# Product's norm: 8-KB pieces, first loads split by channel, the first three units' x gathered during the triangle

## The chip, the cores and the metric

The kernel runs on one core of a Trainium2 chip, in fp32 throughout. The metric is the device time of one execution in microseconds. The runs shown of the kernel before took 1777.58, 1777.96 and 1781.21 us; their median is 1777.96 us.

A core has TensorE (PE), VectorE (DVE), ScalarE (ACT), GpSimd (POOL) and SyncE (SP). Each runs its own instruction list in order. Transfers are started from the lists of SP, ACT and POOL and carried out by 16 DMA engines which all of them share.

## The reference

The input x is one 512 x 512 picture with 64 channels. Two layers follow each other. This change lies in the first one:

```
xn = layernorm(groupnorm(x))                       # over 64 channels
left, right = (xn @ w + b) * mask * sigmoid(...)   # mask[i, j] = m[i] * m[j], m is 0 or 1 per row
out = einsum('bkjd,bkid->bijd', left, right)       # the triangle product, one 512 x 512 product per channel d
out = layernorm(out, onorm_w, onorm_b)             # over d: the product's norm
out = out @ out_w + out_b
x   = x + out * sigmoid(xn @ ogate_w + ogate_b)
```

The second layer is a Fourier convolution that keeps 12 x 12 modes, after another group norm, added to x again. Rows and columns whose m is 0 have a product of zero, and after norm and projection a constant row there.

## The kernel before

At most K = 256 rows have m = 1, and the kernel ranks them first. The path that runs here is `compact`. Its stages, in order of time:

1. A first reading of x for the group norm's sums, and of the 256 x 256 compact part into on-chip memory (to about 300 us of the trace).
2. The sides: left and right are made and stored to DRAM in `left_d` and `right_d`, each [64 channels, 256, 256] (to 445 us).
3. **The triangle** (447 to 619 us): a loop over the 64 channels c. `load_sides(c + 6)` (L865) fetches a channel's two sides, 256 KB each, `turn_sides` (L873, PE) transposes them, `keep_sides` (L879 DVE, L883 ACT) takes them out of PSUM, `product(c)` (L895 PE, L900 DVE) multiplies and masks them, and L903 stores 256 KB to `tri_d` [64, 256, 256]. The sides have five buffers each; the output has four. SP issues the loads and the stores in the order of the code: store of c, then loads of c + 6. POOL has nothing to do in this stage.
4. **The product's norm** (621 to 752 us): `tri_d` holds channels outermost, the norm wants channels innermost. The work goes in 64 steps of 1024 (i, j) pairs. `load_product(q)` (L1025) fetches what two steps need, as two DMAs of 64 channels x 4 KB, into a ring of four buffers that fills place 6. `centered(s)` (L1058, PE) multiplies by a centering matrix and by the output weights at once, which also turns the data. ACT squares the one half (L1078) and copies the other (L1079). DVE sums the squares of two steps (L1083), ACT takes the root for 8 steps (L1089), DVE inverts it (L1263) and scales (L1271), POOL adds the output bias for two steps (L1278), and L1283 stores 512 KB, 4 KB for each partition, to `u_d`.
5. **The units** (750 to 1450 us): 32 units of 64 columns x 128 rows in 8 steps each. `load(k, r)` (L638, an indirect DMA from POOL, two of 1024 KB for each unit, one 8-KB row for each partition) gathers the unit's x; PE transposes and projects it (L1038, L1045), and the gate, the product from `u_d` (`load_u`, L1100, 32 DMAs from SP for each pair of units) and x are joined (L1109, L1113, POOL). L1129 stores the new x to `x1_h`; statistics and the forward transform go beside it.
6. The Fourier modes, and the last pass over x: gather, add, store (from 1450 us).

Stages 4 and 5 are one loop over s, written out by hand under `manual_schedule`: every engine's order is the order of the code, from s = -13 (LEAD) to the end. At step s, `centered` works for step s + 12 and the scaling (L1271) for step s. The gather of unit v + 3 is issued at steps 3 and 6 of unit v, so the gathers of units 0, 1 and 2 are issued in the last 24 steps of the norm. `first` is 8, the number of groups of 8 steps in the norm. A product load waits until PE has done with the buffer it refills; a store to `u_d` waits for POOL's addition; both are in SP's list.

`places` is one on-chip tensor of eight places of 16 KB per partition. x of unit k lies in place `order[k % 5]`, with order = (0, 1, 3, 4, 2). The data of `u_d` for a pair of units lies in place 5 or 6. Place 7 holds smaller things.

## Time and profile before

The profiled execution took 1777.78 us, 0.18 us under the median; its span is 1776.0 us, so 1.8 us lie around the span.

| Engine | busy us in the whole span | share |
|---|---|---|
| PE | 1567.8 | 88% |
| DVE | 1413.7 | 80% |
| ACT | 933.0 | 53% |
| POOL | 936.5 | 53% |

| Stage, us of the span | what runs there | DMA share | GB/s |
|---|---|---|---|
| 450 to 600 | triangle | 0.90 | 301 |
| 600 to 620 | end of the triangle | 0.60 | 209 |
| 640 to 676 | norm | 0.88 | 283 |
| 676 to 711 | norm | 1.02 | 345 |
| 711 to 733 | norm, first gathers of x | 0.92 | 328 |
| 900 to 1000 | units | 0.71 | 248 |
| 1580 to 1776 | last pass | 0.99 | 417 |

DMA share is the mean busy share of the 16 DMA engines in the stretch. The shares over the whole span say little about one stage, since the stages have different limits; the table by stretches of time is the view to begin with, and then the list of one engine's instructions in order of time, with the idle time ahead of each in square brackets and what ended it.

### The profile page before, as it was taken

How to read it: one execution, taken by the hardware profiler on the slowest of the kernel's cores; microseconds unless marked ns; L12 is line 12 of the kernel's file. 1: busy time of each engine (PE TensorE's matmuls, PEld its weight loads, DVE VectorE, ACT ScalarE, POOL GpSimd, SP SyncE). 2: the span in 40 equal slices, each digit the busy share in tenths (PEclk: the TensorE clock that was granted, in tenths of full speed). 3: DMA queues.
4: the chain of work that ended last, by engine and by line, in shares of the span. 5: the costliest groups of instructions: out<-in, count | busy, mean ns of one | idle time of the engine just before them, and what ended most of it. 6: DMA issues, size and time to landing. Idle time of an engine off the chain costs nothing. (4 is left out here: it accounts for less than half of the span.)

```text
span 1776.0 us, 32619 instructions
## 1 busy us (share of the span) xinstructions
PE 1567.8 (88%) x10918; PEld 1242.0 (70%) x10918; DVE 1413.7 (80%) x2982; ACT 933.0 (53%) x1660; POOL 936.5 (53%) x695
## 2 busy tenths in 40 slices
PE   6779799997999978899999999999999977998772
PEld 5667666662899867787888888888888745665341
DVE  7989678887455568688999999999999984865451
ACT  3666566663333266676777777777777742011000
POOL 4666211111000037698999999999999881111110
PEclk9999999999899999899999999999999976555555
DMA  7999278878898789868767767776776699999999
GB/s 281 386 386 388 107 206 227 229 229 245 279 305 303 257 246 347 298 196 296 265 242 257 253 233 259 264 249 239 249 264 244 212 318 400 425 427 427 426 427 385
DMA packets 192593, 518.48 MB, mean 292 GB/s; under 512 B 37664, under 2 KB 104480, under 8 KB 151456
## 3 DMA queue, kind: packets, MB, share of 16 engines
q1 hardware_dynamic: 156112, 295.65, 47.5%
q0 software_dynamic: 32832, 218.45, 33.4%
q10 hardware_dynamic: 3472, 2.20, 0.5%
q8 instruction: 89, 1.46, 0.3%
q14 instruction: 88, 0.72, 0.1%
HBM read 311.60 MB, written 204.60 MB: 291 GB/s over the span
## 5 line engine op out<-in xcount | busy, mean ns | idle before, releaser
L1045 PE MATMUL w_ps<-gate_x,xt_c 128*128 128x128 f32 x2048 | 280.5, 281 | 30.0 <-DVE z_t L1274 28.6
L1113 POOL TENSOR_TENSOR places<-places,z_t 128x1024 f32<-128x1024 f32 x127 | 301.3, 2372 | 8.0
L1045 PEld LDWEIGHTS w_ps<-gate_x,xt_c 128*128 128x128 f32 x2048 | 252.0, 194 | 46.4 <-DVE z_t L1274 44.6
L1045 PE MATMUL c_ps<-center_x,xt_c 128*128 128x128 f32 x2048 | 277.0, 279 | 0.8 <-ACT xt_c L1040 0.4
L1045 PEld LDWEIGHTS c_ps<-center_x,xt_c 128*128 128x128 f32 x2048 | 252.8, 194 | 3.8 <-ACT xt_c L1040 3.0
L1440 PE MATMUL l_ps<-places,rinv 24*128 24x512 f32 x512 | 206.2, 1118 | 29.3 <-DVE places L1447 19.0
L1168 DVE BATCH_NORM_STATS2 stats2c<-places 128x6 f32<-128x128 f32 x1024 | 220.5, 278 | 9.9 <-POOL places L1113 9.9
L1083 DVE TENSOR_REDUCE scratch<-sq_c 128x16 f32<-128x1024 f32 x160 | 194.6, 1216 | 31.1 <-ACT sq_c L1078 16.1
L1221 ACT ACTIVATE z_t<-z_t 128x1024 f32<-128x1024 f32 x128 | 135.5, 1058 | 131.8 <-DVE z_t L1280 131.1
L1440 PEld LDWEIGHTS l_ps<-places,rinv 24*128 24x128 f32 x512 | 119.8, 302 | 110.8 <-DVE places L1447 56.9
L1278 POOL TENSOR_TENSOR z_t<-z_t,bias_row_out 128x1024 f32<-128x1024 f32 x32 | 75.6, 2363 | 226.3 <-PE y_ps L1058 202.1
L1040 ACT ACTIVATE xt_c<-t_ps,ab_xc 128x512 f32<-128x512 f32 x256 | 176.0, 688 | 11.5 <-PE t_ps L1038 10.6
L1274 DVE TENSOR_TENSOR z_t<-w_ps,rs_n 128x512 f32<-128x512 f32 x256 | 172.0, 672 | 6.2 <-PE w_ps L1045 6.1
L1076 ACT ACTIVATE sq_c<-c_ps 128x512 f32<-128x512 f32 x256 | 150.8, 589 | 31.4 <-PE c_ps L1045 30.8
L1280 DVE TENSOR_TENSOR z_t<-z_t,scratch 128x1024 f32<-128x1024 f32 x128 | 156.3, 1221 | 9.9 <-ACT rs_n L1089 3.7
L688 DVE BATCH_NORM_STATS2 stats1c<-x_ps 128x6 f32<-128x512 f32 x256 | 157.1, 682 | 7.7 <-PE x_ps L687 7.4
L1109 POOL TENSOR_TENSOR z_t<-z_t,places 128x1024 f32<-128x1024 f32 x64 | 151.8, 2371 | 14.6 <-ACT z_t L1221 14.4
L1038 PE MATMUL t_ps<-c_ident,places 128*128 128x128 f32 x1024 | 158.4, 278 | 0.0
L1038 PEld LDWEIGHTS t_ps<-c_ident,places 128*128 128x128 f32 x1024 | 118.5, 142 | 51.4 <-issue 51.4
L1447 DVE TENSOR_TENSOR places<-places,l_ps 128x512 f32<-128x512 f32 x176 | 109.3, 682 | 55.2 <-DMA places<-x_h,dst_i 42.1
L1109 POOL TENSOR_TENSOR z_t<-z_t,bias_row_out 128x1024 f32<-128x1024 f32 x63 | 149.4, 2372 | 5.8 <-ACT z_t L1221 5.5
L673 ACT COPY xc<-xg 128x128 f32 x352 | 105.0, 298 | 66.1 <-POOL xc L673 47.1
(214 smaller groups left out, 2557.0 us busy)
## 6 DMA issues: line engine op xcount, KB each, us to landing
x_h<-places SPq DMA_DIRECT2D x64, 1024.0 KB
out_x<-places SPq DMA_DIRECT2D x44, 1024.0 KB
places<-u_d SPq DMA_DIRECT2D x512, 64.0 KB
out_x<-lx_t SPq DMA_DIRECT2D x20, 1024.0 KB
rbc<-rs_d POOLq DMA_DIRECT2D x32, 512.0 KB, 7.1
left_d<-o_c SPq DMA_DIRECT2D x64, 256.0 KB
right_d<-o_c SPq DMA_DIRECT2D x64, 256.0 KB
left_raw<-left_d SPq DMA_DIRECT2D x64, 256.0 KB
```

What stands on the lines that cost most here:

```text
L688: nc.vector.bn_stats(stats[:, 0, 16 * (jc % quarter) + 4 * r + c, :], ps.rearrange("p i k -> p (i k)"))
L1038: nc.tensor.transpose(tps[:, i, :], flat[:, o : o + P], ident)
L1040: nc.scalar.activation(xts[s], tps, AF.Identity, bias=ab1[:, 2:3])
L1045: nc.tensor.matmul(ps[:, 2 * i : 2 * i + 2, :], xts[s][:, i, :], w, start=True, stop=True)
L1076: nc.scalar.activation(sq, cps, AF.Square)
L1083: nc.vector.tensor_reduce(totals[k % 2][:, 8 * (n - 1) : 8 * (n + 1)], sqs.pop(s // 2), AX.X, ALU.add)
L1109: nc.gpsimd.tensor_mul(zs[k, c], zs[k, c], u)
L1113: nc.gpsimd.tensor_add(xr, xr, zs.pop((k, c)))
L1168: nc.vector.bn_stats(st[k // 4][:, g, k % 4, :], x_of(k)[:, :, 2 * g : 2 * g + 2])
L1274: nc.vector.tensor_mul(z[:, 8 * odd : 8 * odd + 8, :], wps, rs)
L1280: nc.vector.tensor_add(z, z, bias_ps["ogate"].unsqueeze(1).to_broadcast([P, 16, C]))
L1440: nc.tensor.matmul(ps.rearrange("p j o -> p (j o)"), rinv[h, b, :], it[h], start=True, stop=True, tile_position=(32 * g, 0),)
```

## The change

- `load_product` fetches pieces twice as long: two DMAs of 64 channels x 8 KB now serve four steps instead of two. The ring of four buffers doubles with it and fills places 5 and 6.
- The scaled and biased product is no longer made in a pool tile of 16 rows per partition but in four halves of places 4 and 2 (`made_t`), 32 rows per partition each, and is stored once for four steps: 16 stores of 1024 KB, 8 KB for each partition, instead of 32 of 512 KB. Scaling on DVE (per step) and bias on POOL (per two steps) keep their number and their amount of work; POOL's addition now runs over two blocks of 8 rows.
- The first four product loads are split by channel. In the last eight rounds of the triangle (c = 56 to 63) one DMA each loads the first 48 of the 64 channels (EARLY = 48), behind that round's store to `tri_d` in SP's list. The loop of the norm loads the other 16 channels where it loaded the whole before.
- The gathers of x for units 0, 1 and 2 move out of the norm's last 24 steps into the triangle: `load_x`, six indirect DMAs from POOL, at rounds c = 4, 14, 24, 34, 44 and 54.
- A product load is issued when its buffer's last reader is issued, as before; with buffers for four steps that is 12 steps ahead of its first use on PE instead of 6.

```diff
@@ -851,6 +851,30 @@
                     own, mask_s.rearrange("p (q b) -> p b q", b=2), ident.unsqueeze(1).to_broadcast([P, 2, P])
                 )
                 nc.vector.tensor_reduce(mask_own, own, AX.X, ALU.add)
+            SIZE = 8
+            LEAD = 13
+            RING = 5
+            EARLY = 3 * C // 4
+            first = K * 2 // 64
+
+            units = [(jc, half) for jc in range(NJ) for half in ((1, 0) if jc < NJ - 1 else (0, 1))]
+            total_g = (first + len(units)) * SIZE
+
+            order = (0, 1, 3, 4, 2)
+
+            def place(i):
+                return places[:, i * 64 * C : (i + 1) * 64 * C].rearrange("p (n c) -> p n c", c=C)
+
+            products_t = [place(5 + i // 2).rearrange("p n c -> p (n c)")[:, i % 2 * 4 * N :][:, : 4 * N] for i in range(4)]
+
+            def load_product(q, halves, low, high):
+
+                for h in halves:
+                    nc.sync.dma_start(
+                        products_t[q % 4][h * C + low : h * C + high],
+                        tri_d.rearrange("c j i -> c (j i)")[low:high, (2 * q + h) * 4 * N : (2 * q + h + 1) * 4 * N],
+                    )
+
             with tc.tile_pool(name="ti", bufs=5) as ip, tc.tile_pool(name="tt", bufs=3) as tp, tc.tile_pool(
                 name="to", bufs=4
             ) as op, tc.tile_pool(name="tpt", bufs=5, space=PSUM) as ps_t, tc.tile_pool(
@@ -902,6 +926,11 @@
                         )
                     nc.sync.dma_start(tri_d[c].rearrange("(p b) i -> p b i", b=2), out_t)
 
+                def load_x(k, r):
+                    jc, half = units[k]
+                    dst = place(order[k])[:, r * JC : (r + 1) * JC]
+                    gather(dst.rearrange("p j c -> p (j c)"), tiles, src_i, 2 * half + r, jc)
+
                 for c in range(4):
                     load_sides(c)
                 for c in range(-2, C):
@@ -913,14 +942,11 @@
                         product(c)
                     if 4 <= c + 6 < C:
                         load_sides(c + 6)
...
+                    if c >= 0 and c % 10 == 4 and c // 20 < 3:
+                        load_x(c // 20, c // 10 % 2)
+                    if c >= C - 8:
+                        load_product((c - C + 8) // 2, (c % 2,), 0, EARLY)
+
             with tc.manual_schedule(), tc.tile_pool(name="late", bufs=1) as lp:
                 sets = chunk_sets(lp, 8)
                 col_basis = lp.tile([P, 4, M2], F32, name="col_basis")
@@ -935,11 +961,6 @@
                 sums = lp.tile([P, MODES, M2], F32, name="sums")
                 nc.vector.memset(sums, 0.0)
 
...
 
                 wide = places[:, 3 * 64 * C : 3 * 64 * C + C * MODES * MODES].rearrange("p (a b) -> p a b", a=C)
                 parts = wide.rearrange("p a b -> p (a b)").rearrange("p (k f) -> p k f", k=2)
@@ -1014,18 +1035,10 @@
                     xts, rss, sqs, us, zs, fs, st = {}, {}, {}, {}, {}, {}, {}
                     last = len(units) - 1
 
-                    products_t = [place(6).rearrange("p n c -> p (n c)")[:, i * 2 * N : (i + 1) * 2 * N] for i in range(4)]
+                    made_t = [place(i)[:, r * JC : (r + 1) * JC] for i in (4, 2) for r in range(2)]
 
                     def x_of(k):
                         return place(order[k % RING])
-
-                    def load_product(q):
-
-                        for h in range(2):
-                            nc.sync.dma_start(
-                                products_t[q % 4][h * C : (h + 1) * C],
-                                tri_d.rearrange("c j i -> c (j i)")[:, (2 * q + h) * 2 * N : (2 * q + h + 1) * 2 * N],
-                            )
 
                     def transpose(s):
                         k, n = divmod(s, SIZE)
@@ -1050,7 +1063,7 @@
                             return times(ps_c, "c_ps", s, center_x)
 
                         ps = ps_y.tile([P, 2, 4, P], F32, name="y_ps")
-                        q, e = divmod(s, 2)
+                        q, e = divmod(s, 4)
                         of = products_t[q % 4][:, e * N : (e + 1) * N].rearrange("p (i k) -> p i k", i=4)
                         for i in range(4):
                             for h in range(2):
@@ -1197,8 +1210,8 @@
                         def held(i):
                             return 0 <= v - i < len(units)
 
-                        while loaded < K // 8 and 2 * loaded - LEAD - 5 <= s:
-                            load_product(loaded)
+                        while loaded < K // 16 and 4 * loaded - LEAD - 11 <= s:
+                            load_product(loaded, range(2), EARLY if loaded < 4 else 0, C)
                             loaded += 1
                         if s + LEAD < total_g:
                             transpose(s + LEAD)
@@ -1238,7 +1251,7 @@
                             i, c = (0, (n - 4) // 2) if n >= 4 else (1, 2 + n // 2)
                             if held(i) and (v - i, c) != (last, 3):
                                 added(v - i, c)
-                        if 0 <= v + 3 < len(units):
+                        if 3 <= v + 3 < len(units):
                             if n == 3:
                                 load(v + 3, 0)
                             if n == 6:
@@ -1263,27 +1276,28 @@
                             nc.vector.reciprocal(factors[(k + 1) % 2] if k + 1 < first else rss[k + 1], rss[k + 1])
                         if wps is not None:
                             c, odd = divmod(n, 2)
-                            if not odd:
-                                z = zp.tile([P, 16, C], F32, name="z_t")
                             if k < first:
+                                made = made_t[s // 4 % 4]
+                                z = made.rearrange("p (h e i) c -> p h e i c", h=2, e=4)
                                 rs = factors[k % 2][:, 16 * c : 16 * c + 16].rearrange("p (h e i) -> p h e i", h=2, e=2)
                                 rs = rs[:, :, odd].unsqueeze(3).to_broadcast([P, 2, 4, C])
-                                nc.vector.tensor_mul(of_pair(z, odd), wps, rs)
+                                nc.vector.tensor_mul(z[:, :, n % 4], wps, rs)
+                                if odd:
+                                    of = made.rearrange("p (h i) c -> p h i c", h=2)[:, :, 8 * (c % 2) : 8 * (c % 2) + 8]
+                                    bias = rows_of["out"].unsqueeze(1).unsqueeze(1).to_broadcast([P, 2, 8, C])
+                                    nc.gpsimd.tensor_add(of, of, bias)
+                                if n % 4 == 3:
+                                    j = 16 * (s // 4)
+                                    nc.sync.dma_start(
+                                        u_d[:, j : j + 16].rearrange("p j r c -> p (j r c)"), made.rearrange("p n c -> p (n c)")
+                                    )
                             else:
+                                if not odd:
+                                    z = zp.tile([P, 16, C], F32, name="z_t")
                                 rs = rss[k][:, 8 * n : 8 * n + 8].unsqueeze(2).to_broadcast([P, 8, C])
                                 nc.vector.tensor_mul(z[:, 8 * odd : 8 * odd + 8, :], wps, rs)
-                            if odd:
-                                if k < first:
-                                    bias = rows_of["out"].unsqueeze(1).to_broadcast([P, 16, C])
-                                    nc.gpsimd.tensor_add(z, z, bias)
-                                else:
+                                if odd:
                                     nc.vector.tensor_add(z, z, bias_ps["ogate"].unsqueeze(1).to_broadcast([P, 16, C]))
-                                if k < first:
-                                    j = JC * k + 8 * c
-                                    nc.sync.dma_start(
-                                        u_d[:, j : j + 8].rearrange("p j r c -> p (j r c)"), z.rearrange("p n c -> p (n c)")
-                                    )
-                                else:
                                     zs[v, c] = z
 
                         if n == 7 and held(0) and v < last:
```

More of the change, by code (lines that the diff above doesn't have):

```diff
@@ L915, in compact @@
                         load_sides(c + 6)
-            SIZE = 8
-            LEAD = 13
-            RING = 5
-            first = K * 2 // 64
-            units = [(jc, half) for jc in range(NJ) for half in ((1, 0) if jc < NJ - 1 else (0, 1))]
-            total_g = (first + len(units)) * SIZE
+                    if c >= 0 and c % 10 == 4 and c // 20 < 3:
+                        load_x(c // 20, c // 10 % 2)
+                    if c >= C - 8:
+                        load_product((c - C + 8) // 2, (c % 2,), 0, EARLY)
             with tc.manual_schedule(), tc.tile_pool(name="late", bufs=1) as lp:
@@ L936, in compact @@
                 nc.vector.memset(sums, 0.0)
-                order = (0, 1, 3, 4, 2)
-                def place(i):
-                    return places[:, i * 64 * C : (i + 1) * 64 * C].rearrange("p (n c) -> p n c", c=C)
                 wide = places[:, 3 * 64 * C : 3 * 64 * C + C * MODES * MODES].rearrange("p (a b) -> p a b", a=C)
```

## The prediction

> **What bounds the kernel now.** I read the table of stretches first, then DVE's own list through the norm, then PE's and POOL's at the place where DVE falls out of step, then the chain from the norm into the units. By stretches (us; PE, PEld, DVE, ACT, POOL busy; granted PE clock, DMA share, GB/s):
>
> ```profile
> 450.00:600.00 150.00, 150.00 (x915) 135.51 (x916) 82.79 (x169) 49.66 (x116) 0.00 (x0) 0.99 0.90 301
> ...
> 640.00:676.00 36.00, 27.84 (x372) 24.29 (x374) 31.00 (x37) 25.88 (x53) 23.62 (x10) 1.00 0.88 283
> 676.00:711.00 35.00, 28.90 (x382) 25.24 (x380) 31.68 (x38) 24.11 (x49) 28.23 (x13) 1.00 1.02 345
> 711.00:733.00 22.00, 16.22 (x126) 13.92 (x126) 10.79 (x13) 10.24 (x21) 12.49 (x7) 0.69 0.92 328
> ```
>
> The triangle is bound by PE, busy 150 of 150 us, with the DMA engines at 0.90. The norm has DVE at 31.68 of 35 us beside DMA engines without a gap. From 711 to 733 DVE is busy for half the time only. DVE's list, where every eighth scaling waits 0.38 us for the root, gives the pace:
>
> ```profile
> 687.24 0.69 DVE L1271 TENSOR_TENSOR z_t<-xt_c,scratch 128x512 f32<-128x512 f32 x1 [0.38 <-ACT rs_n L1089]
> 699.25 0.69 DVE L1271 TENSOR_TENSOR z_t<-xt_c,scratch 128x512 f32<-128x512 f32 x1 [0.38 <-ACT rs_n L1089]
> 711.51 0.69 DVE L1271 TENSOR_TENSOR z_t<-xt_c,scratch 128x512 f32<-128x512 f32 x1 [0.62 <-ACT rs_n L1089]
> ...
> 722.37 1.23 DVE L1083 TENSOR_REDUCE scratch<-sq_c 128x16 f32<-128x1024 f32 x1 [4.04 <-ACT sq_c L1078]
> ...
> 730.00 1.23 DVE L1083 TENSOR_REDUCE scratch<-sq_c 128x16 f32<-128x1024 f32 x1 [5.03 <-ACT sq_c L1078]
> ...
> 733.25 0.69 DVE L1271 TENSOR_TENSOR z_t<-xt_c,scratch 128x512 f32<-128x512 f32 x1 [1.24 <-ACT rs_n L1089]
> ```
>
> Eight steps take 12.0 us, then 12.3, then 21.7. What DVE waits for there is, through ACT, PE, and PE waits for a product load, just when POOL has issued three gathers of 1024 KB:
>
> ```profile
> 708.72 1.04 POOL L638 DMA_INDIRECT places<-in_x,src_i  x1
> 714.84 0.97 POOL L638 DMA_INDIRECT places<-in_x,src_i  x1
> 720.96 0.96 POOL L638 DMA_INDIRECT places<-in_x,src_i  x1 [0.15 <-issue]
> ```
>
> ```profile
> 714.83 0.46 PE L1058 MATMUL y_ps<-both,places 64*128 64x128 f32 x2 [0.74 <-DMA places<-tri_d]
> 717.92 4.58 PE L1058 MATMUL y_ps<-both,places 64*128 64x128 f32 x32 [2.64 <-DMA places<-tri_d]
> 724.18 2.07 PE L1058 MATMUL y_ps<-both,places 64*128 64x128 f32 x14 [1.67 <-DMA places<-tri_d]
> ```
>
> Three gathers are 3.15 MB; at the 345 GB/s of the stretch before they take 9.1 us of all DMA engines, which is the size of the gap (21.7 - 12.0 = 9.7). So 12.0 us for eight steps is DVE's own pace: 4 sums of 1.23, 8 scalings of 0.685 and a reciprocal of 0.56 are 10.96, the rest is the wait for the root and about 0.06 us between instructions. The transfers only just keep up with it, and everything added to them shows.
>
> **The change, part by part.**
>
> *Gathers out of the norm.* Of the six, three cause the gap of 9.7 us. The same starts in DVE's list (650.34, 662.31, 675.22, 687.24, 699.25, 711.51, 733.25, 745.26) span 94.9 us in seven periods; seven at 12.0 are 84.0. Gain 9.7 in the gap and 1.2 in the two other long periods (12.9 and 12.3), where small waits for product loads of 0.3 us add up: **10.9 us**, if DVE's pace is then the bound. ACT needs 0.60 + 0.58 us a step, POOL 2.36 for two, PE about 1.05 a step, all under DVE's 1.5. POOL also saves six issues of about 0.97 us, which cost nothing there, since it waits for DVE in that stretch.
>
> *Do the transfers of the norm keep up?* Eight steps load 2.1 MB and store 2.1 MB in 12.0 us, 349 GB/s; the norm reaches 345 with 4-KB pieces, the last pass 417 with 8-KB pieces. At 345 they fall behind by 0.15 us in each period, 1.2 us in all, and the loads now lead PE by 12 steps, not 6. So I cost this at nothing, covered by that lead. If the cover went, it would be the 1.2 us. [...]
>
> *Fewer, longer DMAs on SP.* 64 product loads become 40, of which 8 move, and 32 stores become 16: 24 x 0.55 and 16 x 0.34 us less in SP's list. SP waits for POOL for 63 us in the norm, so nothing comes of it. A store now stands in front of the next load until POOL has finished four steps; that load still has about 9 steps, some 13 us, until PE needs it, against 9.3 us for a gather's median landing. Nothing, and up to 3 us if PE has to wait at places.
>
> *New buffers.* POOL's addition runs over two blocks of 8 rows instead of one of 16; the same 1024 elements, and up to 3.0 us for two steps (DVE's pace) it would stay hidden. DVE writes four parts of a half place, POOL adds to two parts while DVE writes the next two. The bytes are disjoint. If they were taken as overlapping, DVE would wait 1.2 us (2.36 less a sum of 1.23) once in four steps, 19 us. DVE and ACT write interleaved columns of `q_sb` from 1479.87 and 1479.92 on at the same time, so I take nothing.
>
> *First loads split.* Before, SP issues the first load at 621.08, when the last store has landed; PE starts at 624.61 and runs on from 625.61 after the second, 3.5 us for 256 KB and 1.0 us more for the second. Now the two hold 128 KB each, but the last early loads (384 KB) are on the same DMA engines just before. Between 0 and 1.8 us; I take the middle, **0.8 us gained**. By the Trainium skill (same page, Rules for kernel authors) splitting a transfer over partitions gains nothing because both parts use the same 16 engines; its fixed time of 2 us plus bytes by 436 GB/s would give 2.6 us for 256 KB, where the trace has 3.5, and a gain of 0.3 us for half the bytes. The sum would lose half a microsecond by it.
>
> *Early loads in the triangle.* Eight of 384 KB, 3.1 MB. Between 600 and 620 us the DMA engines are at 0.60, so 8 us are free, and they need about 8 at 400 GB/s. SP waits 78 us for DVE in the triangle, so its 8 x 0.55 us are covered; behind each stands the next round's store. Were a load to wait for the store just ahead of it (1.6 us at 621), SP's round would be 3.0 instead of 2.6 us and the last store 3 us late. I take nothing, as channels 48 and up are not read.
>
> *Six gathers in the triangle.* 6.29 MB. At the stage's own 334 GB/s (301 by 0.90) they need 18.8 us, at 417 they need 15.1. From c = 4 to the end of the loads, 130 us at share 0.91 leave 12 us free. The side loads give a cushion: one issued at 589.76 is used at about 596.0, 6.2 us later, and the first ones landed in 2.8 us on an idle queue; perhaps 2.7 us are left under load. So 14.7 of 15.1 to 18.8 us fit: between 0 and 4 us lost, and 6 if the free share can't be filled. As each gather comes in one burst (2.2 us of arrears against the cushion of 2.7), I take **1.5 us lost**. POOL is idle there, so the issues cost nothing.
>
> *Into the units.* After the last store (752.0) SP waits for it to land, then issues 64 loads of `u_d` from 759.68 on, 0.645 us each, and only then the store of unit 0, which POOL's next gather into the same place awaits:
>
> ```profile
> 759.68 29.99 SPq L1100 DMA_DIRECT2D places<-u_d  x47
> 801.11 3.06 SPq L1129 DMA_DIRECT2D x_h<-places  x4
> 805.87 0.98 POOL L638 DMA_INDIRECT places<-in_x,src_i  x1 [5.18 <-PE c_ps L1045]
> ```
>
> The last store took 7.3 us beside the gathers of 742.72 and 748.59. Alone, 1024 KB should land in about 5 (2.5 us at 417 GB/s plus 2 to 2.5). SP then starts 2.3 us earlier against POOL, and POOL's wait of 5.18 us shrinks by that. Roots of units lie 22 us apart, this one 26.3, so the wait was paid for. **2.3 us gained**, from 0 (a 1024-KB store lands as late as the 512-KB one did) to 4.3.
>
> **Sum**: -10.9 - 0.8 + 1.5 - 2.3 = -12.5 us against the profiled execution's 1777.78 (which is 0.2 under the median): **1765.3 us**. Nothing after the units has slack to swallow it; the last pass follows at the DMA engines' pace and moves as a whole. With the bounds of these terms (gap 9 to 11.2, first loads 0 to 1.8, triangle 4 to 0, units 0 to 4.3) the case's own range is 1760 to 1773.
>
> **Rivals.** (A) *Slower: the triangle pays for the gathers.* PE is at its limit there and the DMA engines at 0.90. If the cushion isn't there and a gather pushes the side loads back by its whole length, six at 3.1 us are 18.8 us, against 14.0 gained: 1782.6. It decides from 14 us of stalls on `left_raw` on. For it: 12 us free and 15 needed. Against it: no wait of PE for a side load in steady state. (B) *Half of it is given back*: 4 to 8 us lost in the triangle and first loads held up behind early loads: about 1772. (C) *No change*: long-pitch 8-KB pieces run slower than 4-KB ones, and the gap moves to other product loads: about 1777. (D) *DVE waits for POOL* in the new buffers: 19 us, so 1784.
>
> **How the numbers follow.** 0.2% (3.6 us) is about what a measurement of this kernel can tell from no change. Chances: forecast 0.72, B 0.12, C 0.07, A 0.06, D 0.03. Faster 0.84 (forecast and B), the same 0.07, slower 0.09. The range reaches from the forecast's own low end to the far side of B, 1759 to 1775; outside lie C, A and D with 0.16 and a few hundredths below.
>
> **What would show it.** Right: DVE's eight-step periods all near 12.0 us and no PE wait for `tri_d` after the first; PE without gaps in the triangle at a DMA share near 1.0; the norm's first matmul about 1 us sooner after the last triangle store; POOL's wait before the gather near 800 us down to about 3 us. Wrong: PE waits for `left_raw` a few us after each gather (A, B); periods of 13 us and more (C); DVE scalings that wait for POOL (D).

## The result, and the profile after

The changed kernel is slower: 1793.18 us median of six runs (1790.56 to 1796.43) against 1777.77 of six runs of the kernel before on the same chip. The ratio is 1.0081, 95% interval [1.0062, 1.0099]; 1765.3 had been forecast. The profiled execution took 1790.56 us with a span of 1788.7, 12.7 longer than before.

The span in stages, each from the end of one instruction to the start of another (us). *Head* is the start of the span to the end of the first product's masking (`tri_t`), *triangle* from there to the end of the last one, *ramp* from there to the first root of the norm (ACT, L1102 after), *norm* the eight periods from the first root to the ninth, *units* from there to the first matmul of the modes (`mixed_ps`), *rest* what follows:

| | head | triangle | ramp | norm | units | rest |
|---|---|---|---|---|---|---|
| before | 456.6 | 162.4 | 20.5 | 105.4 | 724.4 | 306.7 |
| after | 473.8 | 164.2 | 29.2 | 96.1 | 721.4 | 304.0 |
| difference | +17.2 | +1.8 | +8.7 | -9.3 | -3.0 | -2.7 |

The norm gained most of what it was to gain. The head and the ramp, of which the forecast had only small things to say, lost almost three times as much.

**The norm.** DVE's scalings in order of time, in the profile after (start, duration, engine, line, tiles; in brackets the idle time before it and what ended it). The shown ones are the first of an eight-step period, as in the lines shown of before:

```profile
739.17 0.69 DVE L1284 TENSOR_TENSOR places<-xt_c,scratch 128x512 f32<-128x512 f32 x1 [1.51 <-ACT rs_n L1102]
...
751.58 0.69 DVE L1284 TENSOR_TENSOR places<-xt_c,scratch 128x512 f32<-128x512 f32 x1 [0.38 <-ACT rs_n L1102]
...
763.62 0.69 DVE L1284 TENSOR_TENSOR places<-xt_c,scratch 128x512 f32<-128x512 f32 x1 [0.38 <-ACT rs_n L1102]
```

12.4 and 12.0 us; the period of 21.7 is gone, and the longest of the eight, the one before the first line shown, takes 13.4. What PE waited for between the first and the ninth root (in us: total, times, longest), before and then after:

```profile
PE y_ps L1058 <- DMA places<-tri_d: 11.4, 20, 2.6
```

```profile
PE y_ps L1071 <- DMA places<-tri_d: 4.6, 6, 1.4
```

**The head.** POOL's list through the whole triangle, after:

```profile
444.17 1.03 POOL L638 DMA_INDIRECT places<-in_x,src_i  x1 [23.80 <-PE row_out L819]
...
446.60 1.01 POOL L638 DMA_INDIRECT places<-in_x,src_i  x1 [0.30 <-issue]
447.91 0.97 POOL L638 DMA_INDIRECT places<-in_x,src_i  x1 [0.30 <-issue]
449.18 0.93 POOL L638 DMA_INDIRECT places<-in_x,src_i  x1 [0.30 <-issue]
450.42 0.94 POOL L638 DMA_INDIRECT places<-in_x,src_i  x1 [0.31 <-issue]
451.66 0.94 POOL L638 DMA_INDIRECT places<-in_x,src_i  x1 [0.30 <-issue]
```

In the code the six gathers stand at rounds 4, 14, ... 54. In time the first two stand 2.4 us apart and the others 1.3, all of them ahead of the first product. Nothing in POOL's list waits for anything of the triangle, so the rounds of the loop, which order SP, PE, DVE and ACT, don't order POOL. 6.3 MB are then on the DMA engines when the first side loads start. PE's list, after:

```profile
454.60 1.08 PE L897 MATMUL side_ps<-c_ident,left_raw 128*128 128x128 f32 x4 [9.68 <-DMA left_raw<-left_d]
457.64 1.11 PE L897 MATMUL side_ps<-c_ident,right_raw 128*128 128x128 f32 x4 [1.95 <-DMA right_raw<-right_d]
460.77 1.12 PE L897 MATMUL side_ps<-c_ident,left_raw 128*128 128x128 f32 x4 [2.02 <-DMA left_raw<-left_d]
463.82 1.11 PE L897 MATMUL side_ps<-c_ident,right_raw 128*128 128x128 f32 x4 [1.94 <-DMA right_raw<-right_d]
466.97 1.11 PE L897 MATMUL side_ps<-c_ident,left_raw 128*128 128x128 f32 x4 [2.03 <-DMA left_raw<-left_d]
...
469.21 3.62 PE L919 MATMUL tri_c_ps<-right_t,left_t 128*128 128x256 f32 x8
```

And the same place before:

```profile
447.46 1.08 PE L873 MATMUL side_ps<-c_ident,left_raw 128*128 128x128 f32 x4 [4.30 <-DMA left_raw<-left_d]
...
453.36 2.32 PE L895 MATMUL tri_c_ps<-right_t,left_t 128*128 128x256 f32 x8
```

PE gets a side every 3.1 us and waits for each; before, it turned one about every 1.0 us with hardly a wait. The first product starts at 469.21 instead of 453.36. Of the difference of 15.9 us 2.7 are not the burst's, as PE's matmuls ahead of the triangle already stand at 443.26 instead of 440.55. The other 13 are put down to the burst; the experiments below test that. In windows of time (length; PE, PEld, DVE, ACT, POOL busy; granted PE clock, DMA share, GB/s) the head of after reads:

```profile
445.00:450.00 5.00, 0.00 (x0) 0.00 (x0) 1.23 (x3) 0.00 (x0) 4.09 (x6) 0.54 0.89 265
450.00:455.00 5.00, 0.40 (x2) 0.43 (x3) 0.00 (x0) 0.00 (x0) 1.99 (x3) 0.50 1.02 390
455.00:460.00 5.00, 1.80 (x8) 0.99 (x6) 0.69 (x1) 0.85 (x2) 0.00 (x0) 0.50 1.02 419
```

The DMA engines are full, and PE, mostly idle, is granted half its clock: its side transposes take 1.1 us instead of the 0.60 of the steady triangle. The first ones of before were as slow (1.08 in the line shown), but there the first product took 2.32 us, and after 3.62.

**The ramp.** SP's list at the end of the triangle, after (SPq is SP's sequencer; durations are those of issuing):

```profile
625.19 0.32 SPq L873 DMA_DIRECT2D places<-tri_d  x1
630.97 0.32 SPq L927 DMA_DIRECT2D tri_d<-tri_t  x1
632.31 0.32 SPq L873 DMA_DIRECT2D places<-tri_d  x1
632.98 0.32 SPq L927 DMA_DIRECT2D tri_d<-tri_t  x1
637.51 0.32 SPq L873 DMA_DIRECT2D places<-tri_d  x1
...
639.89 0.50 SPq L927 DMA_DIRECT2D tri_d<-tri_t  x1
640.44 19.34 SPq L873 DMA_DIRECT2D places<-tri_d  x11
```

Between an early load (L873) and the store behind it (L927) 5.8 us pass, and between a store and the next early load 4.5; DVE makes a `tri_t` every 2.6. The early load of round 60 (637.51) goes out 7.6 us after that round's `tri_t` is done (629.90). What SP waited for, after (in us: total, times, longest):

```profile
SPq L873 <- DMA tri_d<-tri_t: 7.4, 1, 7.4
...
SPq L927 <- DMA right_raw<-right_d: 5.4, 1, 5.4
SPq L873 <- DMA col_basis<-in_c_table: 4.2, 1, 4.2
```

A store of the product doesn't need a side load, nor an early load the table that ACT's list fetches. Both waits are for a transfer issued long before, so SP seems to be held by something that the DMAs share; we read it as their completion semaphores, but no run here shows that alone. The side load named there seems to be the last one, issued at 623.02 and late itself: PE's last transpose waits for it until 631.05. PE waits 1.4 us in all for the last two sides, and most of the 1.8 us that the triangle lost is that. For the last store to land SP waited 7.4 us, before 1.6, and the loads of the remaining 16 channels that follow are slow:

```profile
648.00:650.00 2.00, 0.00 (x0) 0.00 (x0) 0.00 (x0) 0.00 (x0) 0.00 (x0) 0.50 0.37 102
650.00:652.00 2.00, 0.28 (x1) 0.31 (x2) 0.00 (x0) 0.00 (x0) 0.00 (x0) 0.50 1.19 172
652.00:654.00 2.00, 1.90 (x15) 1.63 (x15) 0.00 (x0) 0.00 (x0) 0.00 (x0) 0.50 0.99 131
```

```profile
651.72 8.52 PE L1071 MATMUL y_ps<-both,places 64*128 64x128 f32 x82 [14.69 <-DMA places<-tri_d]
```

PE's first matmul of the norm comes 13.8 us after the last masking (637.95); before it came 5.6 after (624.61 and 618.97).

### The profile page after: what moved, and what is told of

Read it like the earlier page. It is cut to its first block, busy times and chain, and to the rows that moved or that the text cites. A ratio compares the mean times of both kernels' runs of the same rounds, so it can differ in the third digit from the quotient of the medians.

```text
span 1788.7 us, 32531 instructions
## 1 busy us (share of the span) xinstructions
PE 1563.0 (87%) x10918; PEld 1232.6 (69%) x10918; DVE 1414.0 (79%) x2982; ACT 933.2 (52%) x1660; POOL 935.4 (52%) x695
## 5 line engine op out<-in xcount | busy, mean ns | idle before, releaser
L1454 PE MATMUL l_ps<-places,rinv 24*128 24x512 f32 x512 | 205.6, 1095 | 30.4 <-DVE places L1461 19.1
L1288 POOL TENSOR_TENSOR places<-places,bias_row_out 128x1024 f32<-128x1024 f32 x32 | 75.8, 2368 | 241.6 <-DVE places L1284 233.6
L1122 POOL TENSOR_TENSOR z_t<-z_t,bias_row_out 128x1024 f32<-128x1024 f32 x63 | 149.5, 2372 | 5.2 <-ACT z_t L1234 5.0
```

The costliest lines, as they stand in the source:

```text
L1122: nc.gpsimd.tensor_mul(zs[k, c], zs[k, c], u)
L1454: nc.tensor.matmul(ps.rearrange("p j o -> p (j o)"), rinv[h, b, :], it[h], start=True, stop=True, tile_position=(32 * g, 0),)
```

## The experiments

Every ratio is against runs of the kernel before on the same chip in the same series, with its 95% interval; stages are those of the table above, from one profile each. (The expectations count the triangle from first to last `tri_t` with some 0.4 us more than here, 162.8 for 162.4, and the ramp with up to 0.9 more.) The first `tri_t` starts anywhere from 455.4 to 463.6 us in the profiles of kernels that do the same up to there, so the head of one profile says little. From PE's last work ahead of the triangle (`row_ogate`, L819 in before and after) to the first `tri_t` the profiles agree far better: 29.4 to 29.6 us in the three kernels that let the gathers go together (after, no_early, burst_deep), 13.4 to 15.2 in all the others, before among them. By that the burst costs 14 to 16 us.

### Which part lost: the gathers or the early loads

*no_early*: the changed kernel without the early loads.

```diff
-                    if c >= C - 8:
-                        load_product((c - C + 8) // 2, (c % 2,), 0, EARLY)
...
-                            load_product(loaded, range(2), EARLY if loaded < 4 else 0, C)
+                            load_product(loaded, range(2), 0, C)
```

> The changed kernel without the early part of the first product loads: the loop of the norm loads all 64 channels. Theory that the early loads hurt (they fill the queue ahead of the last side loads and the last store, and the 16-channel rests are slow): the first matmul of the norm comes 6 to 7 us after the last triangle output instead of 14, and the triangle's last rounds lose no time; 8 to 10 us won, about 1784 us. Theory that they help as meant: 1 to 5 us lost, 1794 to 1798 us.

*pieces_only*: no early loads, and the gathers back in the norm; only the 8-KB pieces and the doubled lead are left.

```diff
-                    if c >= 0 and c % 10 == 4 and c // 20 < 3:
-                        load_x(c // 20, c // 10 % 2)
...
-                        if 3 <= v + 3 < len(units):
+                        if 0 <= v + 3 < len(units):
```

> Only the longer pieces: 8-KB loads and stores, buffers in the places, doubled lead; gathers of x back in the norm's last 24 steps, no early loads. If the gap of the norm comes from the gathers' bytes alone, it stays, perhaps 3 us shorter by the longer lead: 1775 to 1778 us. If longer pieces and lead are enough to cover it: 1767 to 1770 us. If 8-KB pieces are slower than 4-KB ones at that pitch: above 1780 us.

*gathers_back*: the gathers back in the norm, but the early loads kept (the second hunk above and the removal of the first, on the changed kernel).

> The changed kernel, with its gathers put back to their place in the norm; 8-KB pieces and early 48-channel loads stay. If the two losses add (gathers 16 us at the head of the triangle, early loads 6 us at its end, against pieces_only), the time is pieces_only's 1771.4 plus 6: 1777, ratio 0.998, with the first product at 453 us as before, the triangle 164.6 us, the ramp 29.6 us. If the early loads hurt only while gathers are near, the time is 1771 to 1773 and the ramp 25 us.

| | ratio | first `tri_t` starts | triangle | ramp | norm |
|---|---|---|---|---|---|
| after | 1.0081 [1.0062, 1.0099] | 472.9 | 164.2 | 29.2 | 96.1 |
| no_early | 1.0045 [1.0031, 1.0059] | 472.7 | 162.4 | 24.1 | 94.9 |
| gathers_back | 1.0003 [0.9988, 1.0017] | 458.7 | 164.4 | 29.3 | 97.9 |
| pieces_only | 0.9949 [0.9931, 0.9968] | 455.7 | 162.4 | 24.4 | 94.8 |

The four make a square. Moving the gathers costs 0.0078 to 0.0096 (14 to 17 us), and the head is where it goes. The early loads cost 0.0036 to 0.0054 (6 to 10 us): 2 in the triangle, 5 in the ramp, 1 to 3 in the norm. gathers_back came out 5 us above its expectation of 1777; 3 of them are in the norm, where the early loads cost more with the gathers beside them, which simple addition left out. And pieces_only, with the gathers at their old place, has a norm of 94.8 us: **the gap is closed without moving a gather**.

### Gathers spread over the triangle

*paced*: the changed kernel, but ahead of each gather POOL copies one column of the newest `tri_t`, so that it waits for its round. *paced_no_early*: the same without early loads.

```diff
-                    out_t = op.tile([P, 2, K], F32, name="tri_t")
+                    out_t = made_c[0] = op.tile([P, 2, K], F32, name="tri_t")
...
+                pace = fc.tile([P, 1], F32, name="pace")
+
                 def load_x(k, r):
+                    nc.gpsimd.tensor_copy(pace, made_c[0][:, 0, 0:1])
                     jc, half = units[k]
```

> The changed kernel, with one addition: before each of the six gathers in the triangle POOL copies one column of that round's output tile, so that the gather cannot start before its round. Burst theory (nothing in the triangle paces POOL, so all six gathers start together at the triangle's head and hold up the first side loads by 13 us): the first triangle product is back at about 12 us after the last sides store, 13 us are won, about 1780 us; the gathers land in the rounds with no wait of PE for a side load above 1 us. Capacity theory (6.3 MB in the triangle cost transfer time wherever they stand): the 13 us only move, PE waits for side loads after each gather, 2 to 3 us six times, 1791 to 1797 us.

> Both together: gathers paced by their rounds, no early product loads; the 8-KB pieces and the doubled lead stay. If burst and early loads are the two losses and add up: 13 + 8 to 10 us won against the changed kernel, about 1769 to 1772 us, faster than before by 6 to 9 us, all of it in the norm's gap. If the gathers cost capacity in the triangle: 1783 to 1788 us.

paced: 1.0052 [1.0031, 1.0073], triangle 182.7 us, ramp 30.0 (its profiled execution, 1804.23 us, was the longest of nine with a median of 1792.39). paced_no_early: 1.0027 [1.0008, 1.0045], triangle 177.8, ramp 24.1. The pacing works: the stretch from `row_ogate` to the first `tri_t` is back at 14.1 and 13.8 us, and in paced_no_early POOL issues a gather every 27 to 30 us. But the cost only moves, as the capacity theory had it for these two kernels: 7 to 9 us behind each gather PE waits for a side. The fourth gather in POOL's list, and PE's list behind it:

```profile
552.18 0.96 POOL L638 DMA_INDIRECT places<-in_x,src_i  x1 [0.50 <-issue]
```

```profile
561.62 0.97 PE L897 MATMUL side_ps<-c_ident,right_raw 128*128 128x128 f32 x4 [2.54 <-DMA right_raw<-right_d]
```

PE's waits in the whole triangle (total, times, longest), and its window:

```profile
PE side_ps L897 <- DMA right_raw<-right_d: 8.4, 6, 2.5
PE side_ps L897 <- DMA left_raw<-left_d: 1.6, 3, 1.0
```

```profile
460.00:625.00 165.00, 154.86 (x924) 136.94 (x923) 84.73 (x174) 49.11 (x114) 6.98 (x12) 0.98 0.92 315
```

The waits come to 10.0 us. The triangle is 15.4 us longer; the other 5 we take for slower work behind the waits (the transposes above took 0.97 us instead of 0.60, the granted clock over the stretch is 0.98 instead of 1.00). That is 2.6 us for each gather, and 1.05 MB at the last pass's 417 GB/s take 2.5: a gather costs its whole length, although the DMA engines are at 0.92 only. The free part of them is there, but the side loads have no lead to use it.

*paced_deep*: paced_no_early with eight buffers for the sides instead of five, and loads nine rounds ahead instead of six.

```diff
-            with tc.tile_pool(name="ti", bufs=5) as ip, tc.tile_pool(name="tt", bufs=3) as tp, tc.tile_pool(
+            with tc.tile_pool(name="ti", bufs=8) as ip, tc.tile_pool(name="tt", bufs=3) as tp, tc.tile_pool(
...
-                    if 4 <= c + 6 < C:
-                        load_sides(c + 6)
+                    if c == -2:
+                        for ahead in range(4, 7):
+                            load_sides(ahead)
+                    if 7 <= c + 9 < C:
+                        load_sides(c + 9)
```

> The paced gathers without early product loads, and the sides of the triangle loaded three rounds further ahead (8 buffers each instead of 5, loads of c + 9 instead of c + 6). Cushion theory (a gather makes the side loads late by about 2.5 us and their lead of 6 us leaves nothing; the free tenth of the DMA time is there): with 7.8 us more lead PE waits for at most one or two side loads, the triangle takes 163 to 167 us instead of 178, about 1771 to 1775 us. Capacity theory (the gathers' 6.3 MB at some 410 GB/s, 15 us, have to be added to the triangle): it takes 173 to 179 us, only the first wait moves later, 1781 to 1787 us.

*burst_deep*: paced_deep without the copies, so that the gathers go out together again.

> paced_deep without the copies that pace the gathers: six gathers written at rounds 4 to 54, side loads nine rounds ahead with eight buffers, no early loads. If POOL's list is not held by the loop, the six gathers go out together near 445 us, more side loads (seven pairs) compete with them, the first product comes 10 to 15 us later than in paced_deep, the triangle itself takes 162.8 us, and the time is 8 to 15 us above paced_deep's 1775.8. If instead the deeper side loads were what made paced_deep cheap, the burst costs under 4 us and the time is 1776 to 1780.

paced_deep: 0.9957 [0.9944, 0.9970], triangle 162.4, the length without any gather. Its window, to be set against the one above:

```profile
465.00:625.00 160.00, 159.38 (x973) 143.07 (x971) 92.04 (x195) 51.72 (x120) 6.99 (x12) 1.00 0.94 329
```

PE is busy 159.4 of 160 us beside 329 GB/s. burst_deep: 1.0038 [1.0023, 1.0052], 14 us above paced_deep, with the first `tri_t` at 474.65 instead of 462.05 and the triangle itself at 162.4. Lead doesn't help against the burst, and pacing alone doesn't help against the shortage of lead; both together make the gathers free in the triangle. Set against pieces_only (0.9949), which leaves them in the norm, nothing is gained by that.

### What closes the gap, and what the 8-KB pieces do

*lead_only*: the kernel before with product loads 12 steps ahead, in pieces of 4 KB (a ring of eight instead of four). The scaled product goes to the four halves of places, as in the change, but is stored in 512-KB pieces as before. Gathers at their old place, no early loads. The four halves hold eight pieces of the scaled product where the kernel before had four; before, DVE's scalings waited for roots alone between the first and the ninth root, so that this second difference is unlikely to count, but it was not tested by itself.

```diff
-                    products_t = [place(6).rearrange("p n c -> p (n c)")[:, i * 2 * N : (i + 1) * 2 * N] for i in range(4)]
+            products_t = [place(5 + i // 4).rearrange("p n c -> p (n c)")[:, i % 4 * 2 * N :][:, : 2 * N] for i in range(8)]
...
-                        while loaded < K // 8 and 2 * loaded - LEAD - 5 <= s:
+                        while loaded < K // 8 and 2 * loaded - LEAD - 11 <= s:
```

> The pieces stay at 4 KB as before the change (64 product loads of 256 KB in a ring of eight, 32 stores of 512 KB), only the ring is doubled, so that a load leads PE by 12 steps; gathers in their old place, no early loads, first load of 256 KB as before. If the lead closes the norm's gap: all periods near 12 us, root of the first unit about 94 us after the first root, and a first matmul as early as before; 1766 to 1769 us. If the longer pieces close it (more bytes a second): a gap of 5 to 10 us stays, 1773 to 1778 us.

0.9958 [0.9945, 0.9971]; norm 94.7 us, ramp 20.6, and no wait of PE for `tri_d` between the first and the ninth root. In windows, 710 to 742 being the stretch in which five of the six gathers are issued:

```profile
680.00:710.00 30.00, 21.99 (x300) 20.23 (x298) 26.82 (x33) 20.34 (x41) 23.37 (x10) 0.91 1.02 349
710.00:742.00 32.00, 27.91 (x311) 25.77 (x310) 28.61 (x35) 24.73 (x46) 29.59 (x16) 0.98 0.94 332
```

The same gathers on equally full DMA engines, and DVE works at its pace, 28.6 of 32 us. Against lead_only, the 8-KB pieces of pieces_only change the norm by nothing and make the ramp 3.8 us longer (24.4). The reading was that PE then waits for twice the bytes before it can start. Two tries to mend that:

*first_by_columns*: pieces_only, with the first load in two parts of 4 KB for each channel.

```diff
+                parts = 2 if q == 0 else 1
+                size = 4 * N // parts
+                for part in range(parts):
+                    for h in halves:
+                        o = (2 * q + h) * 4 * N + part * size
```

> Only the longer pieces, with the very first load cut by columns: the first two steps' 256 KB of each half, then the next two's. In the version with only the longer pieces the norm's first root came 3.8 us later than before, since PE waited for 512 KB and then for 512 KB more. If the size of the first load is that: the first root at about 639.5 to 640.5 us of the span, 1768 to 1769 us. If something else (the rate of the loads in the ramp) sets it: 1770 to 1772 us.

*two_queues*: the same, and the upper half of the partitions loaded from ACT's list for the first three loads.

```diff
+                        (nc.scalar if h and q < 3 else nc.sync).dma_start(
```

> The same, and the second half (partitions 64 to 127) of the first three product loads issued from ACT's list instead of SP's. In the ramp the loads run at 222 GB/s with the DMA engines at share 1.02. If that is because one half of 64 partitions at a time can only be written at about half of the 417 GB/s, two queues write both halves at once: 300 to 400 GB/s in the ramp, the first matmuls about 1 us sooner, 1766 to 1768 us. If the reading side sets the rate (rows 256 KB apart): still 220 GB/s and no gain, 1768 to 1770 us.

first_by_columns: 0.9961 [0.9947, 0.9974], ramp 22.1, back by 2.3 of the 3.8, so the size of the first load is most of it; the ratio is no better than that of pieces_only (0.9949). two_queues: 0.9956 [0.9939, 0.9973], not told apart from it; ramp 24.6 and norm 98.8 in its profile, which was the longest of six executions (1786.69 us with a median of 1777.39).

### The early loads: place, volume or partitions

*lead_deep*: lead_only with the gathers as in paced_deep (paced, sides nine rounds ahead).

> The before kernel with doubled lead of the product loads in 4-KB pieces (as in lead_only), and besides it the six gathers in the triangle, each behind a copy that waits for its round, with side loads nine rounds ahead (as in paced_deep). Theory (what costs is lead and piece size, not the gathers' place): triangle 162.8 us from first to last tri_t, last tri_t to first root 21 us, eight periods of the norm 94.7 us, the wait of POOL for a gather at the start of the units 4.5 us instead of 7.0; time 2 to 3 us under lead_only, 0.994 of the before kernel. Rival (gathers in the triangle always cost): triangle 165 us or more, time at or above lead_only's 0.996.

*early_deep*: lead_deep, with the 48-channel parts of the first four product loads in the triangle. Since pieces are of 4 KB, that is half the volume of the change.

```diff
+                    if c in (54, 55, 56, 57):
+                        load_product(c - 54, 0, EARLY)
...
-                            load_product(loaded)
+                            load_product(loaded, EARLY if loaded < 4 else 0, C)
```

> lead_deep, and the 48-channel parts of its first four product loads (each of two 4-KB pieces a channel) are issued in rounds 54 to 57, after the last side loads; the 16-channel rests after the last store. Theory A (the early loads of the changed kernel hurt because they met the last side loads and because half of an 8-KB load went to few partitions): triangle unchanged at 162.8 us, ramp from last tri_t to first root 17 to 19 us instead of 21, time 2 to 4 us under lead_deep. Theory B (a load into 16 partitions is slow whatever its volume, and the early loads in SP's list hold up the last stores): ramp 21 to 25 us, time equal to lead_deep or up to 4 us above it.

*early_late*: the same eight loads, one in each of rounds 56 to 63, the place they have in the change.

```diff
-                    if c in (54, 55, 56, 57):
-                        load_product(c - 54, 0, EARLY)
+                    if c >= C - 8:
+                        load_product((c - C + 8) // 2, 0, EARLY, (c % 2,))
```

> early_deep with its eight early loads one in each of rounds 56 to 63, as the changed kernel has them, instead of two in each of rounds 54 to 57. If it is their place just ahead of the last stores that costs in the changed kernel, the last tri_t comes 1 to 3 us later than 162.4 us after the first and the ramp grows from 19.6 to 22 us or more; time 3 to 6 us above early_deep. If place doesn't matter and only the volume (384 KB against 192 KB each) does, it equals early_deep within 2 us.

*early_long*: paced_deep with the 8-KB early loads of the change, in rounds 54 to 57.

> paced_deep (8-KB pieces, side loads nine rounds ahead) with its eight early loads of 384 KB two in each of rounds 54 to 57. If volume is what costs: 3.1 MB into 48 partitions need about 17 us, to round 62 or so, the last stores queue behind them, the ramp is 23 us or more, and the time is at or above paced_deep's 0.996. If only the collision with the last side loads and stores cost, the ramp falls from 24.8 us to 20 to 22 and the time is 3 to 5 us under paced_deep.

*pitch* and *early_pitch*: lead_deep and early_deep with channels 257 KiB apart in `tri_d`.

```diff
-        tri_d = dram.tile([C, K, K], F32, name="tri_d")
+        tri_d = dram.tile([C, K + 1, K], F32, name="tri_d")
...
-                    nc.sync.dma_start(tri_d[c].rearrange("(p b) i -> p b i", b=2), out_t)
+                    nc.sync.dma_start(tri_d[c, :K].rearrange("(p b) i -> p b i", b=2), out_t)
```

> lead_deep with one more row for each channel in tri_d, so that channels lie 257 KiB apart instead of 256 KiB; same bytes, same DMAs. If the pitch is what holds the product loads at 236 to 244 GB/s in the ramp (rule of the Trainium skill, DMA: Bandwidth & Descriptors, Latency and other measured facts), these loads rise to 300 GB/s and more, the ramp from last tri_t to first root falls from 22.7 us to about 19, and the time falls 3 to 6 us under lead_deep. If it is the 64 partitions into which each load writes (SBUF - State Buffer, Door 1), the ramp stays at 236 to 244 GB/s, 21 to 23 us long, and the time is lead_deep's 0.993.

> early_deep with the same 257-KiB pitch. If the pitch costs nothing: time equal to early_deep's 0.990, ramp 19.6 us. If it costs: ramp 17 us or less and 3 us and more under early_deep.

| | early loads | ratio | triangle | ramp | norm |
|---|---|---|---|---|---|
| lead_deep | none | 0.9931 [0.9912, 0.9949] | 162.4 | 21.8 | 94.7 |
| pitch | none | 0.9933 [0.9915, 0.9952] | 162.4 | 21.0 | 94.9 |
| early_deep | 8 x 192 KB, rounds 54-57 | 0.9903 [0.9884, 0.9921] | 162.4 | 18.8 | 95.6 |
| early_pitch | 8 x 192 KB, rounds 54-57 | 0.9914 [0.9895, 0.9933] | 162.4 | 19.1 | 94.8 |
| early_late | 8 x 192 KB, rounds 56-63 | 0.9929 [0.9911, 0.9947] | 162.4 | 19.7 | 94.8 |
| paced_deep | none (8-KB pieces) | 0.9957 [0.9944, 0.9970] | 162.4 | 24.2 | 94.8 |
| early_long | 8 x 384 KB, rounds 54-57 | 0.9992 [0.9978, 1.0006] | 169.9 | 20.4 | 97.8 |

*Volume* is what costs, or the piece length that doubles with it: 192 KB are 48 pieces of 4 KB, 384 KB 48 of 8 KB, and no run separates the two. With 192 KB each the triangle keeps its 162.4 us wherever the loads stand, and the ramp is 18.8 to 19.7 us instead of the 20.6 to 21.8 of lead_only, pitch and lead_deep. The late place, for which one theory had 3 to 6 us, shows 0.9 in the ramp and nothing in the triangle; the intervals of early_late and early_deep overlap, so a difference of that size stays open. With 384 KB each the stores behind the loads are late. In the last 40 us of early_long's triangle DVE waits for a store to free its `tri_t`, four times, 10.9 us in all,

```profile
DVE tri_t L924 <- DMA tri_d<-tri_t: 10.9, 4, 3.7
```

and the triangle is 7.5 us longer. Against paced_deep the ramp is 3.8 shorter, not longer as that theory had it, and the norm 3.0 longer: 6.7 in sum, where the ratios have 0.0035, 6 us. So the split itself does what it is for, and its size takes back more, in the triangle.

*Pitch* doesn't set the rate of the product loads; the number of partitions may. Twelve us of the ramp of lead_deep, and then of pitch:

```profile
630.00:642.00 12.00, 11.05 (x148) 9.84 (x145) 4.91 (x4) 10.16 (x19) 0.00 (x0) 0.90 1.03 239
```

```profile
632.00:644.00 12.00, 11.71 (x158) 10.41 (x158) 4.91 (x4) 10.55 (x19) 0.00 (x0) 0.91 1.04 239
```

239 GB/s both, with the DMA engines fully busy. These are loads alone, each into 64 partitions; once stores are in the stream the rate goes to the 349 shown for lead_only. The first theory leans on the Trainium skill (DMA: Bandwidth & Descriptors, Latency and other measured facts), which has 207 GB/s for a pitch of 512 KiB where it calls 214 the full rate; its low figures begin at 2 MiB, and 256 KiB is not in its row. The second theory is near what the Trainium skill says (SBUF — State Buffer, Door 1: The DMA port swizzle): 64 partitions reach half of the 16 ports, about 218 GB/s, and 16 partitions a quarter of them, about 109. In windows with loads into 64 partitions alone and a DMA share of 0.98 to 1.07 the rate is 207 to 250; for the 16-channel rests it is 131 to 172 at shares of 0.99 to 1.19. Both are in part above the page's figures. A further section of that page ("Can I just issue two DMAs to hit both halves?") has 6% gained by two loads on the two halves. In two_queues the rate was

```profile
632.00:636.00 4.00, 3.60 (x44) 3.30 (x44) 1.23 (x1) 2.15 (x4) 0.00 (x0) 0.81 1.04 254
636.00:640.00 4.00, 2.01 (x28) 1.63 (x26) 1.23 (x1) 2.05 (x4) 0.00 (x0) 1.00 1.00 266
```

so 254 to 266 against 234 and 227 in the same 8 us of first_by_columns, some 13% more, and no time from it. That is far from the 417 of the last pass, though all 128 partitions were being written. No run changed the number of partitions alone, so what holds these loads is not shown.

**The best version** is early_deep: 1762.64 us median against 1780.31 for the kernel before in its series, 0.9903 [0.9884, 0.9921], 18 us. It has the doubled lead, pieces of 4 KB, paced gathers in the triangle with sides nine rounds ahead, and early loads of half the volume. Its interval, from four executions, overlaps that of lead_deep, so what the early loads add rests on the ramps more than on the times.

## Why the prediction was wrong

*Gathers out of the norm (10.9 us gained).* Right in size: 9.3 us after, 10.7 where no early load disturbs it (94.7 of 105.4). The period of 12.0 us is DVE's own, as read. PE's waits for `tri_d` fell from 11.4 us to 4.6, and to nothing in lead_only. But the reason was half of it. "The transfers only just keep up with it, and everything added to them shows" left out that a load further ahead has time to spare; lead_only closes the same gap with the gathers at their old place.

*Do the transfers keep up (nothing).* Right where no early loads are in the way: between the first and the ninth root PE waits for `tri_d` once in no_early, 0.4 us, and not at all in paced_deep and lead_only. The 4.6 us of after come with the early loads. The row pitch is no hindrance: pitch and early_pitch show that 256 or 257 KiB make no difference here.

*Fewer DMAs (nothing), new buffers (nothing).* Right; DVE's scalings wait for the roots (4.2 us in the norm of after) and not for POOL, so rival D is out. But the longer pieces were not free elsewhere: the ramp pays 3.8 us, most of it for the first load of twice the size. That term was missing, because the working only asked for SP's time and the norm's rate.

*First loads split (0.8 us gained) and early loads (nothing).* Wrong: 6 to 10 us lost instead. "SP waits 78 us for DVE in the triangle, so its 8 x 0.55 us are covered" counted SP's issue time, not that a load in SP's list can be held until an older transfer has landed, and the store behind it with it. "They need about 8 at 400 GB/s" took a rate that loads of this shape don't have here; at the 207 to 250 measured for 64 partitions the 3.1 MB need 13 us or more. The doubt stood in the text as a last store 3 us late, and was not carried to the sum. With half the volume the idea holds, at 1 to 3 us of the ramp.

*Six gathers in the triangle (1.5 us lost).* This is the step that failed, twice over. First, "each gather comes in one burst" was priced as six bursts 26 us apart; they were one burst of 6.3 MB, since nothing holds POOL at round c. "POOL is idle there, so the issues cost nothing" was the sentence to stop at: an idle engine with nothing to wait for runs ahead to the end of its list. Second, the "cushion of 2.7" us between a side load's landing and its use wasn't there: paced_no_early lost 2.6 us for each gather, 15.4 in all. That is rival A, which had 18.8 for the same mechanism and a chance of 0.06. It was weighed down by "no wait of PE for a side load in steady state", which says that the loads are in time, not by how much. The changed kernel itself lost its time in one burst at the head, which neither the forecast nor a rival had. By the ratios both ways cost 14 to 17 us, the one at the head, the other along the triangle.

*Into the units (2.3 us gained).* POOL's wait of 5.18 us ahead of its gather near 800 us became 3.88 after; the units took 3.0 less in that profile. The wait moved the right way, but the 2.3 us are not shown: the units take 721.4 to 727.1 us in the profiles of all the kernels, and the wait went from 2.45 (early_deep) to 7.30 (pieces_only, gathers in the norm).

Sum by the profiles: head +17.2 (2.7 of it from ahead of the burst), triangle +1.8, ramp +8.7, norm -9.3, units and rest -5.7. The last figure is within what these stages differ by from profile to profile anyway (721.4 to 727.1 and 303.9 to 310.3 us), so nothing was lost or surely gained after the norm.

## What to carry to other kernels

A place in a loop orders an instruction only against what its engine waits for: work given to an idle engine starts when its list allows, so give it a wait that belongs to its round, and ask how many bytes it then sets loose at once. A free share of the DMA engines was of use here only once the stream beside the new transfers had more lead; no wait in the trace doesn't measure lead, the distance between landing and use does, and adding buffers to the stream that must not be late is worth trying before moving the one that disturbs it. And before loads are pulled ahead of the last stores of a stage, count their bytes at the rate that loads of the same shape have in the trace, not at the highest rate found in it.

## What the runs showed of the hardware

- The product loads into 64 partitions keep all DMA engines busy (share 0.98 to 1.07) at 207 to 250 GB/s, those into 16 partitions (share 0.99 to 1.19) at 131 to 172; the last pass moves 417 at 0.99. A DMA share near 1 so doesn't say that the bytes flow at the highest rate.
- In SP's list a DMA waited, by the profile, 4.2 and 5.4 us for the landing of unrelated older transfers, one of them issued from ACT's list. Why was not tested.
- Where PE had stood idle its granted clock was 0.50 to 0.54 (445 to 460 us of after) and work was slow: a side transpose took 1.1 us instead of 0.60, the first product 3.62, the next 1.89.
- A copy of one column on POOL, 0.19 us, was enough to hold a gather at its round (paced_no_early: one every 27 to 30 us instead of every 1.3).
